# Bucketed quads of a graph network's scatter-add: 16 groups of 392 nodes in place of 8 of 784, four row bands of the matrix array at once, parts by truncation

## The chip, the cores and the metric

One core of a Trainium2 chip runs the whole program. The metric is the time of one execution on the device, in microseconds, as the median of several runs. The core has five engines with queues of their own: TensorE (PE in the profile; its weight loads are PEld), VectorE (DVE), ScalarE (ACT), GpSimd (POOL) and the queue that issues most DMAs, SyncE (SP). TensorE writes into PSUM, which is held here as eight banks of 128 x 512 float32: four under the tag A and four under the tag B.

## The reference, cut to what matters

6250 nodes with 128 features, 200000 edges sorted by `dst`. A layer norm and a relu, a matrix, then for each edge a filter from its 20 attributes, the product of that filter and the row of node `dst`, summed at node `src`; then two more matrices, and the input is added.

```python
h = jnp.maximum(_layernorm(x, axis=-1), 0.0)
x_in = h @ W_in
W_ij = shifted_softplus(f_ij @ W_f1 + b_f1) @ W_f2 + b_f2
W_ij = W_ij * f_ij_cutoff
x_ij = x_in[dst] * W_ij
out = jax.ops.segment_sum(x_ij, src, num_segments=N_ATOMS)
return x + shifted_softplus(out @ W_o1 + b_o1) @ W_o2 + b_o2
```

`src` is random over all nodes, so the sum over edges is the hard part: every edge adds a row of 128 float32 numbers at a random node.

## The kernel before

The edges are taken in quads: four chunks of 128 edges, 512 in all. There are 391 quads. One loop (from `s1_pe(0)` on, near line 903) runs over iterations i and issues, in an order written out by hand, one stage of each of several quads: the filter's first layer of quad i + 1, its softplus of quad i, the gather of node rows and the second layer of quad i - 1 (`xg`, `W`), the product `m` of i - 1, and the sum within each chunk of i - 2. Everything else is hung into that loop by `at(i, point, function)`; the points of an iteration are, in this order: L (loads), A0 (ScalarE), D0 (VectorE), D1 (VectorE), A1, then after the main products PE2 (TensorE), A2, D2 (VectorE) and S (scatters). Each engine works its own queue strictly in the order in which instructions were issued.

A quad's 512 rows of `m` reach their nodes in one of two ways.

A direct quad compares the edges of each chunk with each other (`s1_eq`, line 308), sums the rows of equal nodes by a float32 matmul (`s3_pe`, `pp`, line 356), copies the result (`s3_copy`, line 364), computes where to write (`s3_idx`), and scatters four times 128 rows into one of four accumulators in HBM by an indirect DMA that adds (`scatter`, line 399, issued by GpSimd).

A bucketed quad (`mpq`, every third quad from quad 5 on, 128 of them) is summed on TensorE without HBM. The nodes are cut into 8 groups of 784 (`GRP`, `GN`). `rank_group` to `rank_slot` give each edge of eight quads at a time a slot: its group's 64 slots (`CAP`) in order of rank, or one of 64 overflow slots (`OVC`). Then, for each quad:

- `m` is cut into three bfloat16 parts whose sum is `m`: `part_cast` (ScalarE, line 493) rounds `m`, `part_rem` (VectorE, line 499) takes the remainder, `part_cast` rounds that, `part_rem` (line 504) takes the rest. The parts and three columns for the node's place (`ext`) stand side by side in `pt`, 387 columns.
- `perm_oh` (line 485) makes the 0/1 matrix `pm` from edge to slot, `permute` (line 510) multiplies, in four blocks of 128 slots, and `perm_out` (ScalarE, line 517) copies each block from PSUM to `ms`.
- `over_pe` (lines 531 to 533) sums the parts of the edges in overflow slots, and for each two quads `over_idx` to `over_scatter` write these by one scatter.
- Four quads share an accumulation (`RND`). `unit_oh` (line 586) makes, for one block of slots, the 0/1 matrix from slot to place in the group (784 columns); `unit_pe` (line 601) multiplies each part of `ms` with it, for the block's two groups in two 64-row bands of the array, into two PSUM banks, in two halves h of 392 columns; `unit_evac` (lines 611 and 613, VectorE) adds each bank to `accT`, the sum over all bucketed quads in SBUF.

A half unit is 4 quads x 3 parts x 2 bands = 24 matmuls. The halves run at PE2 of iterations q + 5 and q + 6 of the next round's quads, and are added to `accT` at D0 of the iteration after. Permutes run at PE2 of q + 4 and q + 5, two blocks each.

Around the loop: the node table is built in small groups during the first 60% (`prep_*`), the attributes are split and written back to HBM (`fb_*`), and near the end the first accumulator is loaded, transposed and added to `accT` (`r0_load`, line 832, through tiles of the tag `pm`; `r0_tp`, line 839). After the loop the other three accumulators are loaded, summed and added, and the last two matrices follow (lines 1020 on).

A loop behind line 957 would redo edges that found no slot; its count of trips is computed on the chip, and it is 0 when every overflow fits.

Of the kernel before, what the change touches and what calls it, by code (L numbers as in the profile page):

```python
# [20 lines left out]
P = 128  # L21
SC = 1024
SEG = 512
GRP = 8
CAP = 64
# [3 lines left out]
MPGAPS = (3,)  # L29
MPEND = 4  # L30
RND = 4
RKQ = 8
PW = 388
# [9 lines left out]
def tile_gnn(ctx: ExitStack, tc: tile.TileContext, x, fB, cT, srcT, srcr, dstr, win_, wf1, wf2, bias, bo1c, wo1,  # L43
# [25 lines left out]
    HN = GN // 2  # L69
    mpq = sorted_quads(NQ)  # L70
    mpi = {q: n for n, q in enumerate(mpq)}
    scat = [0] * (NQ + 12)
# [45 lines left out]
    iot = cp.tile([P, GN], F16, name="iot")  # L118
# [171 lines left out]
    def s1_ln(q):  # L290
        l = wk.tile([P, 512], F32, tag="l", name="l")
        nc.scalar.activation(l, st[q]["e"], AF.Ln, bias=half, scale=0.5)  # L292
        st[q]["l"] = l
# [34 lines left out]
    def s2_pe_w(q):  # L328
        W = ps.tile([P, 4, P], F32, tag="A", name="W", bufs=4)
        nc.tensor.matmul(W.rearrange("p c f -> p (c f)"), ones3[:, :P], b2rep.rearrange("k c f -> k (c f)"),  # L330
                         start=True, stop=False)
        for c in range(4):
            nc.tensor.matmul(W[:, c, :], st[q]["a"][:, c * P:(c + 1) * P], w2, start=False, stop=(c == 3))  # L333
        st[q]["W"] = W
# [7 lines left out]
    def s2_m(q):  # L342
        m = ms[q % 3]
        nc.vector.tensor_tensor(m[:, :, :P], st[q]["W"], st[q]["xc"], op=ALU.mult)  # L344
        st[q]["m"] = m
# [63 lines left out]
    def rank_group(r):  # L409
# [16 lines left out]
        ext = wk.tile([P, 4 * RKQ, 3], BF16, tag="ext", name="ext")  # L426
        nc.vector.tensor_copy(ext[:, :nc4, 0], loc[:, :nc4])
        nc.vector.tensor_tensor(ext[:, :nc4, 1], loc[:, :nc4], ext[:, :nc4, 0], op=ALU.subtract)
        nc.vector.tensor_copy(ext[:, :nc4, 2], cnt[:, :nc4])
# [59 lines left out]
    def part_cast(q, k):  # L489
        if k == 0:  # L490
            mp.setdefault(q, {})["pt"] = wk.tile([P, 4, PW], BF16, tag="pt", name="pt")
        src_ = st[q]["m"][:, :, :P] if k == 0 else mp[q]["rem"]
        nc.scalar.copy(mp[q]["pt"][:, :, k * P:(k + 1) * P], src_)  # L493

    def part_rem(q, k):
        pt = mp[q]["pt"]
        if k == 1:
            rem = wk.tile([P, 4, P], F32, tag="rem", name="rem", bufs=1)
            nc.vector.tensor_tensor(rem, st[q]["m"][:, :, :P], pt[:, :, :P], op=ALU.subtract)
            mp[q]["rem"] = rem  # L500
            r, j = divmod(mpi[q], RKQ)
            nc.vector.tensor_copy(pt[:, :, 3 * P:3 * P + 3], rk[r]["ext"][:, 4 * j:4 * j + 4])
        else:
            nc.vector.tensor_tensor(pt[:, :, 2 * P:3 * P], mp[q]["rem"], pt[:, :, P:2 * P], op=ALU.subtract)
            del st[q]

    def permute(q, s):
        t = ps.tile([P, 512], F32, tag="B", name="pq", bufs=4)
        for c in range(4):
            nc.tensor.matmul(t[:, :3 * P + 3], mp[q]["pm"][:, c, s * P:(s + 1) * P], mp[q]["pt"][:, c, :3 * P + 3],  # L510
                             start=(c == 0), stop=(c == 3))
        mp[q]["q", s] = t

    def perm_out(q, s):
        if s == 0:
            mp[q]["ms"] = wk.tile([P, 4, PW], BF16, tag="ms", name="mst", bufs=2 * RND)
        nc.scalar.copy(mp[q]["ms"][:, s, :3 * P + 3], mp[q].pop(("q", s))[:, :3 * P + 3])  # L517

    def perm_loc(q):
        lo = wk.tile([P, 4], F32, tag="lo", name="lo", bufs=2 * RND)  # L520
        nc.vector.tensor_tensor(lo, mp[q]["ms"][:, :, 3 * P], mp[q]["ms"][:, :, 3 * P + 1], op=ALU.add)
        mp[q]["lo"] = lo

    def over_pe(q):
# [3 lines left out]
        for c in range(4):  # L528
            w = mp[q]["pm"][:, c, GRP * CAP:]
            pt = mp[q]["pt"][:, c]  # L530
            nc.tensor.matmul(o[:, :P + 3], w, pt[:, 2 * P:3 * P + 3], start=(c == 0), stop=False)  # L531
# [4 lines left out]
    def over_out(q):  # L536
        h = mpi[q] % 2 * OVC
        mo = mos[mpi[q] // 2 % 2]
        nc.scalar.copy(mo[h:h + OVC, :P + 3], mp[q].pop("po")[h:h + OVC, :P + 3])

    def over_idx(q):
        mo = mos[mpi[q] // 2 % 2]
        so = sp_.tile([P, 2], F32, tag="ovs", name="ovs", bufs=2)
        nc.vector.scalar_tensor_tensor(so[:, 0:1], mo[:, P + 2:P + 3], float(GN), mo[:, P:P + 1], op0=ALU.mult,
                                       op1=ALU.add)
        nc.vector.tensor_tensor(so[:, 1:2], so[:, 0:1], mo[:, P + 1:P + 2], op=ALU.add)
        dg = wk.tile([P, P], F32, tag="dg", name="dg", bufs=1)
        nc.vector.tensor_scalar(dg, idt, so[:, 1:2], None, op0=ALU.mult)
# [7 lines left out]
    def over_eq(q):  # L556
        eq = wk.tile([P, P], F32, tag="oeq", name="oeq", bufs=1)
        nc.vector.tensor_scalar(eq, mp[q].pop("row")[:, :P], mp[q]["so"][:, 1:2], None, op0=ALU.is_equal)  # L558
        mp[q]["eq"] = eq

    def over_sum(q):
        t = ps.tile([P, 512], F32, tag="B", name="osum", bufs=4)
        nc.tensor.matmul(t[:, :132], mp[q]["eq"], mos[mpi[q] // 2 % 2][:, :132], start=True, stop=True)
        mp[q]["sum"] = t

    def over_copy(q):
        s = sp_.tile([P, 132], F32, tag="os", name="os", bufs=2)
        nc.scalar.copy(s, mp[q].pop("sum")[:, :132])  # L568
        mp[q]["os"] = s

    def over_ji(q):
        s, so = mp[q]["os"], mp[q]["so"]
        jd = sp_.tile([P, 2], F32, tag="ojd", name="ojd", bufs=2)
        nc.vector.tensor_scalar(jd[:, 0:1], so[:, 1:2], trash, None, op0=ALU.subtract)
        nc.vector.scalar_tensor_tensor(jd[:, 1:2], s[:, 131:132], wgt2, jd[:, 0:1], op0=ALU.is_lt, op1=ALU.mult)
# [7 lines left out]
    def unit_oh(r, s):  # L583
        for q in mpq[r * RND:(r + 1) * RND]:
            so = wk.tile([P, GN], BF16, tag="so", name="so", bufs=RND + 1)
            nc.vector.tensor_scalar(so, iot, mp[q]["lo"][:, s:s + 1], None, op0=ALU.is_equal)  # L586
# [4 lines left out]
    def unit_pe(r, s, h):  # L591
        ts = []
        for g in range(2):
# [3 lines left out]
        for q in qs:  # L597
            for k in range(3):
                for g in range(2):
                    v = slice(g * CAP, (g + 1) * CAP)  # L600
                    nc.tensor.matmul(ts[g][:, :HN], mp[q]["ms"][v, s, k * P:(k + 1) * P],  # L601
                                     mp[q]["oh"][v, h * HN:(h + 1) * HN], start=(q == qs[0] and k == 0),
                                     stop=(q == qs[-1] and k == 2))
        un[r, s, h] = ts

    def unit_evac(r, s, h):
        for g, t in enumerate(un.pop((r, s, h))):
            o = (2 * s + g) * GN + h * HN
            v = accT[:, o:o + HN]
            if r == 0:  # L610
                nc.vector.tensor_copy(v, t[:, :HN])
            else:
                nc.vector.tensor_tensor(v, t[:, :HN], v, op=ALU.add)  # L613
# [19 lines left out]
    def src_cols(a, b):  # L633
        t_ = wk.tile([P, b - a], I32, tag="pt", name="srci")
        nc.sync.dma_start(t_, srcT[:, a:b])
        nc.gpsimd.tensor_copy(srcT_sb[:, a:b], t_)
# [6 lines left out]
    with tc.manual_schedule():  # L643
# [9 lines left out]
        nc.gpsimd.iota(iot, pattern=[[1, GN]], base=0, channel_multiplier=0, allow_small_or_imprecise_dtypes=True)  # L653
# [7 lines left out]
        src_cols(0, CE)  # L661
        nc.sync.dma_start(w2, wf2)
# [5 lines left out]
        ones3 = cp.tile([3, 512], BF16, name="ones3")  # L668
# [9 lines left out]
        def split3(dst, src, rows, c0, tag):  # L678
            p = wk.tile([rows, 3, P], BF16, tag="e", name=f"{tag}_parts")
            r = wk.tile([rows, P], F32, tag="l", name=f"{tag}_rem")  # L680
# [54 lines left out]
        for i in range(3):  # L735
# [3 lines left out]
        for mo_ in mos:  # L739
            nc.vector.tensor_copy(mo_[:, 131:132], wgt)  # L740
# [16 lines left out]
        def late_cols():  # L757
            w = -(-(EP // P - CE) // 2)
            src_cols(CE, CE + w)
            src_cols(CE + w, EP // P)  # L760
            nc.sync.dma_start(cT_sb[:, CE:], cT[:, CE:])

        at(3 if spread else 0, "D2", rel_ext, 0, rel0)
        if CE < EP // P:
            at(7, "L", late_cols)

        def half_piece(k, tag, **kw):
            lo, hi = k * SEG, (k + 1) * SEG
            r = rel(1, lo, hi, tag, **kw)
            src_cast(1, lo, hi, nc.vector, tag, **kw)  # L770
            rel_ext(1 + k, r)

        kw = {"bufs": 2 * RND}
        for k in range(2):
            i = 2 + 2 * k if spread else 0
            at(i, "L", lambda k=k: load_idx(1, k * SEG, (k + 1) * SEG, "ms", **kw))
            at(i + 2 if spread else i, "D2", lambda k=k: half_piece(k, "ms", **kw))
# [4 lines left out]
        for g in range(1, NG):  # L782
# [15 lines left out]
            at(t0 + 3, "D1", prep_rm, g)  # L798
# [57 lines left out]
        at(mid + 7 if spread else 0, "D1", late_add)  # L856
# [3 lines left out]
        for g in range(len(tgroups)):  # L860
# [3 lines left out]
            at(min(i + 3, NQ + 4), "D1", r0_add, g)  # L864
        for r in range(-(-len(mpq) // RKQ)):
            i = mpq[RKQ * r]
            at(i - 4, "D2", rank_group, r)
            at(i - 2, "PE2", rank_count, r)
            at(i - 1, "D1", rank_own, r)
            at(i, "PE2", rank_over, r)  # L870
            at(i + 1, "D1", rank_slot, r)
        for q in mpq:
            at(q + 2, "A2", part_cast, q, 0)
            at(q + 2, "D2", part_rem, q, 1)
            at(q + 2, "D2", perm_oh, q)
            at(q + 3, "A1", part_cast, q, 1)
            at(q + 3, "D2", part_rem, q, 2)
            for s in range(4):
                at(q + 4 + s // 2, "PE2", permute, q, s)
                at(q + 5 + s // 2, "A0", perm_out, q, s)  # L880
            at(q + 4, "PE2", over_pe, q)
            at(q + 5, "A0", over_out, q)
            at(q + 6, "D1", perm_loc, q)
            if mpi[q] % 2:
                at(q + 5, "D2", over_idx, q)
                at(q + 6, "PE2", over_row, q)
                at(q + 7, "D1", over_eq, q)
# [5 lines left out]
        for r in range(len(mpq) // RND):  # L893
            for u in range(8):
                s, h = divmod(u, 2)
                n = RND * (r + 1) + s
                k = (mpq[n] + 5 if n < len(mpq) else last + 7 + 2 * s) + h
                if h == 0:
                    at(k - 1, "D2", unit_oh, r, s)
                at(k, "PE2", unit_pe, r, s, h)  # L900
                at(k + 1, "D0", unit_evac, r, s, h)

        s1_pe(0)
        for i in range(max(NQ + 6, last + 16)):
# [54 lines left out]
    with tc.For_i(0, trips, 1) as ci:  # L959
# [10 lines left out]
        sb = wk.tile([P, P], I32, bufs=1, tag="rem", name="fsb")  # L970
# [27 lines left out]
        nc.tensor.matmul(W, ones3[:, :P], b2rep[:, 0, :], start=True, stop=False)  # L998
# [8 lines left out]
        s = wk.tile([P, P], F32, tag="l", name="fs")  # L1007
# [230 lines left out]
```

## Time and profile before

| | |
|---|---|
| median of 3 runs | 2316.84 us (2315.01 to 2321.35) |
| the profiled execution: time, span | 2317.84 us, 2315.7 us |
| mean granted TensorE clock | 0.974 |
| iterations of the loop | 391 and 11 that finish |
| scatters (line 399) | 1051 of direct quads, 64 of overflow |
| unit matmuls (line 601) | 6144 |
| permute matmuls (line 510) | 2048 |
| adds and copies to accT (lines 613, 611) | 496 and 16 |

A busy time is the union of an engine's instructions; the gap between two start times tells what an instruction costs its engine when the next one follows at once. [...]

### The profile page before, as it was taken

The numbers are of one execution on the slowest core, as the hardware profiler recorded it, in microseconds if no ns is written. First come the engines' busy times: TensorE is split into PE (matmuls) and PEld (weight loads), VectorE is DVE, ScalarE is ACT, GpSimd is POOL, SyncE is SP. The second block draws the span as 40 slices with busy tenths as digits, with TensorE's granted clock in tenths as the row PEclk, the third lists the DMA queues.
The fourth block names the chain that finished last, engine by engine and source line by source line (L and its number), as shares of the span: only waits on it lengthen the run. The fifth ranks groups of instructions, "written<-read, shape, count | busy, mean of one in ns | idle before, by whom it ended". The sixth has DMA issues, their size and how long they took to land.

```text
span 2315.7 us, 53016 instructions
## 1 busy us (share of the span) xinstructions
PE 2142.7 (93%) x18065; PEld 1492.7 (64%) x18065; DVE 1976.5 (85%) x5339; ACT 1843.1 (80%) x4486; POOL 1844.8 (80%) x1159
## 2 busy tenths in 40 slices
PE   4589999999999999999999999999999999999886
PEld 3466666666666666666666666666666666666554
DVE  6589888999989999998989889888888888898574
ACT  4498888888888888888888888878888888887534
POOL 3677788888888888888888888888888888887564
PEclk8699999999999999999999999999999999999997
DMA  8887777777777777777777777777777677776537
GB/s 302 210 185 140 143 145 149 145 143 152 151 142 137 160 146 140 151 146 150 138 155 142 135 141 145 148 133 141 134 145 141 140 147 140 140 147 136 117 41 222
DMA packets 399056, 345.26 MB, mean 149 GB/s; under 512 B 87656, under 2 KB 313806, under 8 KB 398784
## 3 DMA queue, kind: packets, MB, share of 16 engines
q1 hardware_dynamic: 237136, 265.37, 38.2%
q0 software_dynamic: 161360, 76.42, 33.8%
q8 instruction: 142, 2.33, 0.4%
q14 instruction: 130, 1.06, 0.2%
q10 hardware_dynamic: 288, 0.07, 0.0%
HBM read 198.15 MB, written 143.57 MB: 148 GB/s over the span
## 4 chain that ended last, share of the span: by engine, by line
PE 63%; ACT 20%; DVE 7%; DMA 4%; issue 3%; SPq 1%; POOL 1%; ACTq 0%; DVEq 0%; POOLq 0%
PE un L601 20%; PE W L333 11%; PE pp L356 9%; PE pq L510 8%; ACT xc L339 5%; PE xg L325 3%; PE W L330 3%; ACT e L287 3%; ACT e L286 3%; PE z L281 2%; ACT pt L493 2%; DMA acc<-s,ji 2%; PE po L531 2%; ACT l L292 2%; PE po L533 1%
## 5 line engine op out<-in xcount | busy, mean ns | idle before, releaser
L399 POOL DMA_INDIRECT acc<-s,ji x1051 | 1703.5, 1621 | 396.2 <-issue 177.3
L601 PE MATMUL un<-so,mst 64*128 64x392 bf16 x6144 | 597.1, 332 | 47.2 <-ACT os L568 17.7
L601 PEld LDWEIGHTS <-mst 64*128 64x128 bf16 x6144 | 321.3, 95 | 278.0 <-issue 95.3
L339 ACT ACTIVATE xc<-xg,cT_sb 128x128 f32<-128x128 f32 x1564 | 443.1, 363 | 52.1 <-PE xg L325 48.7
L333 PE MATMUL W<-w,a 128*128 128x128 f32 x3128 | 461.1, 291 | 0.0
L333 PEld LDWEIGHTS W<-w,a 128*128 128x128 f32 x3128 | 385.7, 194 | 93.4 <-issue 92.7
L510 PE MATMUL pq<-pt,pm 128*128 128x387 bf16 x2048 | 380.4, 327 | 1.0 <-DVE oeq L558 0.9
L314 DVE SCALAR_TENSOR_TENSOR a<-z,l 128x512 f32<-128x512 f32 x391 | 267.3, 684 | 80.3 <-ACT l L292 80.3
L344 DVE TENSOR_TENSOR m<-W,xc 128x512 f32<-128x512 f32 x391 | 267.1, 683 | 58.9 <-ACT xc L339 56.8
L364 ACT COPY s<-pp 128x258 f32<-128x258 f32 x526 | 192.4, 382 | 156.0 <-PE pp L356 142.8
L613 DVE TENSOR_TENSOR accT<-un,accT 128x392 f32<-128x392 f32 x496 | 256.2, 557 | 62.7 <-PE un L601 60.0
L356 PEld LDWEIGHTS pp<-m,eq 128*128 128x128 f32 x2104 | 283.7, 196 | 13.5 <-ACT s L364 2.0
L292 ACT ACTIVATE l<-e,con 128x512 f32<-128x512 f32 x391 | 282.2, 722 | 12.7
L356 PE MATMUL pp<-m,eq 128*128 128x129 f32 x2104 | 284.6, 279 | 1.4 <-ACT s L364 1.4
L517 ACT CAST mst<-pq 128x387 bf16<-128x387 f32 x512 | 238.7, 502 | 59.3 <-PE pq L510 59.2
L510 PEld LDWEIGHTS <-pm 128*128 128x128 bf16 x2048 | 198.4, 97 | 115.6 <-issue 1.7
L287 ACT ACTIVATE e<-e 128x512 f32<-128x512 f32 x391 | 246.5, 630 | 12.5
L286 ACT ACTIVATE e<-z 128x512 f32<-128x512 f32 x391 | 241.7, 618 | 9.4 <-PE z L281 7.9
L586 DVE TENSOR_SCALAR so<-iot,lo 128x784 bf16<-128x784 f16 x512 | 192.4, 437 | 0.1
L485 DVE TENSOR_SCALAR pm<-iot,pos 128x576 bf16<-128x576 f16 x512 | 165.7, 385 | 22.5 <-PE rtp L839 22.5
L308 DVE TENSOR_TENSOR eq<-sb,srcT_sb 128x512 f32<-128x512 int16 x263 | 179.1, 681 | 0.0
L325 PE MATMUL xg<-wn,oh 126*128 126x128 bf16 x1564 | 157.5, 224 | 16.1 <-DVE a L314 10.4
(157 smaller groups left out, 2567.4 us busy)
## 6 DMA issues: line engine op xcount, KB each, us to landing
sb<-src SPq DMA_DIRECT2D x195, 256.0 KB
rb<-reld SPq DMA_DIRECT2D x195, 252.0 KB
ft<-fsd SPq DMA_DIRECT2D x195, 240.0 KB
fsd<-f SPq DMA_DIRECT2D x49, 480.0 KB
acc<-s,ji POOLq DMA_INDIRECT x1051
fb<-in_fB_dram SPq DMA_DIRECT2D x49, 320.0 KB
fsd<-f SPq DMA_DIRECT2D x49, 320.0 KB
wn<-tab SPq DMA_DIRECT2D x391, 31.5 KB
```

Of the source, the lines that this page charges most:

```text
L286: nc.scalar.activation(e, st[q]["z"], AF.Abs)
L287: nc.scalar.activation(e, e, AF.Exp, scale=-1.0)
L292: nc.scalar.activation(l, st[q]["e"], AF.Ln, bias=half, scale=0.5)
L314: nc.vector.scalar_tensor_tensor(a, st[q]["z"], 0.0, st[q]["l"], op0=ALU.max, op1=ALU.add)
L333: nc.tensor.matmul(W[:, c, :], st[q]["a"][:, c * P:(c + 1) * P], w2, start=False, stop=(c == 3))
L339: nc.scalar.mul(xc[:, c, :], st[q]["xg"][:, c, :], cT_sb[:, 4 * q + c:4 * q + c + 1])
L344: nc.vector.tensor_tensor(m[:, :, :P], st[q]["W"], st[q]["xc"], op=ALU.mult)
L356: nc.tensor.matmul(pp[:, c, :129], st[q]["eq"][:, k, :], m[:, k, :129], start=True, stop=True)
L399: nc.gpsimd.indirect_dma_start(out=accs[k][:, :], out_offset=bass.IndirectOffsetOnAxis(ap=ji, axis=0), in_=s, in_offset=None, compute_op=A ...
L510: nc.tensor.matmul(t[:, :3 * P + 3], mp[q]["pm"][:, c, s * P:(s + 1) * P], mp[q]["pt"][:, c, :3 * P + 3], start=(c == 0), stop=(c == 3))
L601: nc.tensor.matmul(ts[g][:, :HN], mp[q]["ms"][v, s, k * P:(k + 1) * P], mp[q]["oh"][v, h * HN:(h + 1) * HN], start=(q == qs[0] and k == 0) ...
L613: nc.vector.tensor_tensor(v, t[:, :HN], v, op=ALU.add)
```

## The change

It touches the bucketed quads, how many there are, and the buffers around them.

- 16 groups of 392 nodes with 32 slots each (`GRP`, `CAP`); a block of 128 slots holds four groups, so a unit multiplies four bands of 32 rows into four PSUM banks at once, all four under the tag B. There are no halves.
- Three quads of eight are bucketed (gaps 3, 2, 3): 144. Six quads share an accumulation, so there are 24 rounds of four units, each 6 x 3 x 4 = 72 matmuls of 392 columns.
- Parts by truncation: `m` of a bucketed quad is written straight into a float32 `pt`; the upper 16 bits of a float32 are its truncated bfloat16, so a part is a view of every second bfloat16 of the float32 tile (`high`). ScalarE's two casts are gone; the two remainders stay on VectorE and write float32. The moving operand of `permute` and `over_pe` has a step of two elements.
- A node's place in its group needs one column in place of two (it is stored less 196, and 196 is added back in `perm_loc` and `over_ji`), so `ext` has two columns and `pt` 386.
- `perm_oh` runs at q + 1 (before q + 2), both remainders at q + 2, permutes at q + 3 and q + 4 (before q + 4 and q + 5), `perm_loc` in two halves; units run at q + 2 of those quads of the next round that follow at a gap of three, an iteration in which the direct product `pp` is missing because quad q is bucketed.
- Rank steps run one iteration apart and some of them move from D1 to D0, as do `over_eq`, `prep_rm`, `late_add` and `r0_add`.
- `l` is written over `e`; two `m` buffers instead of three; the late halves of the indices are loaded through the tag `pm` at iterations 1 and 2 (before 2 and 4) and cast at 3 and 5 (before 4 and 6); two late blocks of `srcT` are loaded at iterations 11 and 13 (before both at 7) and narrowed by VectorE (before GpSimd).

```diff
-GRP = 8
-CAP = 64
+GRP = 16
+CAP = 32
-MPGAPS = (3,)
+MPGAPS = (3, 2, 3)
-RND = 4
+RND = 6
-PW = 388
+PW = 386
...
     def s2_m(q):
-        m = ms[q % 3]
+        m = part_new(q) if q in mpi else ms[plain[q] % 2]
...
-    def part_cast(q, k):
-        if k == 0:
-            mp.setdefault(q, {})["pt"] = wk.tile([P, 4, PW], BF16, tag="pt", name="pt")
-        src_ = st[q]["m"][:, :, :P] if k == 0 else mp[q]["rem"]
-        nc.scalar.copy(mp[q]["pt"][:, :, k * P:(k + 1) * P], src_)
+    def high(t):
+        return t.bitcast(BF16)[:, :, 1::2]
+
+    def part_new(q):
+        mp.setdefault(q, {})["pt"] = wk.tile([P, 4, PW], F32, tag="pt", name="pt")
+        return mp[q]["pt"]
 
     def part_rem(q, k):
         pt = mp[q]["pt"]
+        a = pt[:, :, (k - 1) * P:k * P]
+        nc.vector.tensor_tensor(pt[:, :, k * P:(k + 1) * P], a, high(a), op=ALU.subtract)
...
-            nc.tensor.matmul(t[:, :3 * P + 3], mp[q]["pm"][:, c, s * P:(s + 1) * P], mp[q]["pt"][:, c, :3 * P + 3],
+            nc.tensor.matmul(t[:, :PW], mp[q]["pm"][:, c, s * P:(s + 1) * P], high(mp[q]["pt"][:, c:c + 1, :PW])[:, 0],
                              start=(c == 0), stop=(c == 3))
...
-    def unit_pe(r, s, h):
+    def unit_pe(r, s):
         ts = []
-        for g in range(2):
+        for g in range(4):
             t = ps.tile([P, 512], F32, tag="B", name="un", bufs=4)
             ts.append(t)
         qs = mpq[r * RND:(r + 1) * RND]
         for q in qs:
             for k in range(3):
-                for g in range(2):
+                for g in range(4):
                     v = slice(g * CAP, (g + 1) * CAP)
-                    nc.tensor.matmul(ts[g][:, :HN], mp[q]["ms"][v, s, k * P:(k + 1) * P],
-                                     mp[q]["oh"][v, h * HN:(h + 1) * HN], start=(q == qs[0] and k == 0),
-                                     stop=(q == qs[-1] and k == 2))
+                    nc.tensor.matmul(ts[g][:, :GN], mp[q]["ms", s // 2][v, s % 2, k * P:(k + 1) * P], mp[q]["oh"][v],
+                                     start=(q == qs[0] and k == 0), stop=(q == qs[-1] and k == 2))
...
         for r in range(len(mpq) // RND):
-            for u in range(8):
-                s, h = divmod(u, 2)
-                n = RND * (r + 1) + s
-                k = (mpq[n] + 5 if n < len(mpq) else last + 7 + 2 * s) + h
-                if h == 0:
-                    at(k - 1, "D2", unit_oh, r, s)
-                at(k, "PE2", unit_pe, r, s, h)
-                at(k + 1, "D0", unit_evac, r, s, h)
+            nxt = [mpq[n] + 2 for n in range(RND * (r + 1), min(RND * (r + 2), len(mpq))) if mpq[n] - mpq[n - 1] == 3]
+            for s in range(4):
+                k = nxt[s] if nxt else last + 6 + 2 * s
+                at(k - 1, "D2", unit_oh, r, s)
+                at(k, "PE2", unit_pe, r, s)
+                at(k + 1, "D0", unit_evac, r, s)
```

## The prediction

> **What bounds the kernel now.** I read the page first, then the busy time by stage, then TensorE's and VectorE's timelines. All sums below stand against the profiled execution: span 2315.7 us, 2317.84 us as a time, 1.0 us above the median 2316.84.
>
> ```profile
> span 2315.7 us, 53016 instructions
> PE 2142.7 (93%) x18065; PEld 1492.7 (64%) x18065; DVE 1976.5 (85%) x5339; ACT 1843.1 (80%) x4486; POOL 1844.8 (80%) x1159
> PE 63%; ACT 20%; DVE 7%; DMA 4%; issue 3%; SPq 1%; POOL 1%; ACTq 0%; DVEq 0%; POOLq 0%
> ```
>
> ```profile
> 0.00:150.00 150.00, 87.21 (x531) 66.36 (x532) 92.38 (x257) 88.27 (x218) 84.32 (x69) 0.83 0.85 241
> 150.00:2100.00 1950.00, 1882.78 (x16220) 1309.23 (x16218) 1746.66 (x4763) 1644.15 (x4022) 1629.19 (x1004) 0.99 0.73 145
> 2100.00:2316.00 216.00, 172.73 (x1319) 117.07 (x1318) 137.40 (x323) 110.64 (x248) 131.27 (x88) 0.90 0.59 125
> ```
>
> The columns are length, then busy time of PE, PEld, DVE, ACT, POOL. From 150 to 2100 us PE is busy 1882.78/1950 = 96.6%, DVE 89.6%, ACT 84%, POOL 84%: TensorE sets the pace, VectorE is 136 us behind it, and the granted clock is 0.99. Busy overcounts streaming, but start times agree:
>
> ```profile
> 1002.00 2.17 PE L601 MATMUL un<-so,mst 64*128 64x392 bf16 x24
> 1004.10 0.40 PE L325 MATMUL xg<-wn,oh 126*128 126x128 bf16 x4
> ...
> 1005.96 1.05 PE L356 MATMUL pp<-m,eq 128*128 128x129 f32 x8
> 1006.85 1.48 PE L510 MATMUL pq<-pt,pm 128*128 128x387 bf16 x8
> 1008.27 0.24 PE L531 MATMUL po<-pt,pm 128*64 128x131 bf16 x1
> ...
> 1009.06 0.40 PE L325 MATMUL xg<-wn,oh 126*128 126x128 bf16 x4
> ```
>
> From start to next start: half a unit (24 matmuls) takes 2.10 us, the product pp 0.89, two permuted slot blocks 1.42, the overflow block 0.79. In the first, two 64-row bands take 12 x 175 ns for 392 columns; a full-height permute of 387 columns takes 1.42/8 = 177 ns. So the second band costs nothing beside the first.
>
> **TensorE, part by part.**
> - Accumulation: 256 half units x 2.10 = 537.6 us go. 96 units of 72 matmuls come, in 18 groups of four row bands. Two bands already stream at the price of one, so I give four the same 175 ns: 3.15 us a unit, 302.4 in all, **-235**. Ends: no dearer than that, or two bands at a time, 36 x 175 = 6.30 us, 604.8 in all (+67). I take the first, the nearer row being two bands that overlap wholly.
> - 16 more bucketed quads x (2 x 1.42 + 0.79) = **+58**; 16 fewer direct products x 0.89 = **-14**.
> - Ranks 16 to 18 groups at twice the width, and 8 more overflow pairs: at most **+12** (orow and osum are busy 26.8 + 25.0 us for 64 now, so 0.8 us a pair).
> - The permutes now read every second bf16 of a float32 tile. No row has a strided moving operand. Ends: nothing, or half the stream rate, 144 x (16 x 177 ns + 12 x 66 ns) = +522. The nearest row is pp, whose float32 operand has a 4-byte step too and takes 0.89/8 = 111 ns a row of 129 columns against 66 ns for bf16 po; but it does other arithmetic and comes as two instructions a product, so it decides little. I take nothing.
>
> Sum **-179**, to 1964 us.
>
> [...]
>
> **VectorE.**
>
> ```profile
> 1008.33 1.41 DVE L586 TENSOR_SCALAR so<-iot,lo 128x784 bf16<-128x784 f16 x4
> 1009.66 0.21 DVE L379 SCALAR_TENSOR_TENSOR jf<-s,con,jd 128x4 f32<-128x4 f32 x1
> ...
> 1013.73 0.68 DVE L499 TENSOR_TENSOR rem<-m,pt 128x512 f32<-128x512 f32 x1
> 1014.33 0.17 DVE L502 COPY pt<-ext 128x12 bf16<-128x12 bf16 x1
> 1014.40 1.20 DVE L485 TENSOR_SCALAR pm<-iot,pos 128x576 bf16<-128x576 f16 x4
> 1015.52 1.03 DVE L613 TENSOR_TENSOR accT<-un,accT 128x392 f32<-128x392 f32 x2
> 1016.47 0.34 DVE L299 TENSOR_SCALAR oh<-rb,con 126x512 bf16<-126x512 bf16 x1
> ```
>
> By starts: so 1.33/4 = 0.333 us at 784 columns, pm 1.12/4 = 0.28 at 576, so 392 columns cost 0.28 - 184 x 0.000255 = 0.233; an accT add 0.475; a remainder 0.60.
> - accT 512 to 384: **-61**. so 512 x 0.333 to 576 x 0.233: **-36**.
> - Remainders 256 to 288: **+19**; pm +64 x 0.28 = **+18**; lo 128 to 288 at 0.16: **+25**; eq and index work of 16 quads at 0.60 + 0.38: **-16**.
> - Ranks: five operations widen by 256 elements, 0.27 us each (0.60 against 0.475 for 120 columns); 18 x 1.33 and two groups of 5 us more: **+34**. Overflow and narrowing srcT on DVE instead of POOL: **+4**.
>
> Sum **-13**: VectorE is not relieved.
>
> **ScalarE and GpSimd.**
>
> ```profile
> L493 ACT CAST pt<-m 128x512 bf16<-128x512 f32 x128 | 80.6, 630 | 23.8 <-POOL srcT_sb L636 23.8
> L493 ACT CAST pt<-rem 128x512 bf16<-128x512 f32 x128 | 77.6, 607 | 24.1 <-DVE rem L499 24.1
> ```
>
> Both casts go (-158), 64 more mst copies come (238.7/512 each, +30), s loses 32 of 0.37 (-12), others +5: ACT **-135**. Scatters fall from 1115 to 987 + 72 = 1059: at 1.62 us **-91** on POOL. Both lie beside TensorE and are worth nothing alone; without that cover each ACT microsecond would be paid.
>
> **What is late next.** In the middle stage PE loses its share of 179, some 172, to 1711 us; DVE stays near 1735. So VectorE ends last, by a hair. At the 96.6% that PE reaches now, DVE would need 1796 us for the 1950 (-154). But two engines 1.4% apart wait on each other in turn, and the order adds a coupling: a unit takes all four B banks of PSUM. It is queued where no pp is due (two iterations after a quad), so its banks wait only for ACT's last copies of pq and po (2 x 0.47 + 0.26 = 1.2 us), under xg, W, z (1.86 us, from 1004.10 to 1005.96). Behind the unit on PE stand the next xg, W, z, again 1.86 us, then pp, which waits for the first of four accT adds (1.9 us in all), first in DVE's next iteration. Cover and need are about equal, so a late DVE now stops PE. I take 95%: 1735 / 0.95 = 1826, **-124**.
>
> Moved steps: half_load's four DMAs on SP go one and three iterations earlier and late_cols' two source columns four to six later, their copy passing from POOL's queue to DVE's; SP spends 0.35 to 0.5 us on an issue (sb, rb, ft in its timeline), under zeroing transfers and table loads that fill those iterations; I price this at nothing, 2 us without that cover. At the end accs[0] comes back through tiles that share tag pm, and pm now lives from q+1 to q+4 instead of q+2 to q+4; its issue already blocks SP:
>
> ```profile
> 2119.35 15.85 SPq L832 DMA_DIRECT2D r0t<-acc  x2
> ```
>
> 0 to +20 for that; I take **+5**, as only some of the 13 loads meet a pm. Span 2315.7 - 124 + 5 = 2197, as a time 2199, against the median **2198**. Own range: DVE at 98% (-180) gives 2135, DVE at 92% (-64) with +20 gives 2271.
>
> **Rivals.**
> - D, TensorE stays the bound with its whole gain: 2316 - 179 + 5, **2142**. For it: PE reaches 96.6% today with DVE at 90%. Against: DVE's unchanged sum.
> - C, the four-bank unit turns into a wait. If DVE comes 0.8 us late at each of 96 units, PE stands 77 us: 2198 + 77 = **2275**. For it: PE un already ends 60.0 us of DVE idle time at L613, so they run in step. Against: all hooks sit where a pp is missing.
> - A, on the other side: the stride slows the permutes. At half rate 2316 - 179 + 522 = **2659**; it decides from a permute of 177 + 179/2304 us, 255 ns. For it: no row shows such a read. [...]
> - B, bands run two at a time: 604.8 - 302.4 more, **2440**; decides from 279 ns a group. Against: the wholly hidden second band.
> - The drop path (an edge over a full bucket starts the repair loop) doesn't start: counted over the inputs, a bucketed quad has at most 57 edges over 32 in its group, and 64 places for them.
>
> **How the numbers follow.** Main 0.68, D 0.08, C 0.13, A 0.07, B 0.04. Predicted 2198. The range 2130 to 2285 takes in the main case's ends, D and most of C, some 0.82. A measurement tells 0.3% (7 us) from no change. Faster 0.87 (main, D, nearly all of C), same 0.02, slower 0.11 (A, B).
>
> **What would show it.** Starts of un four at a time, some 175 ns apart, a unit of 3.1 to 3.3 us (B: 6.3); pq still 177 ns (A: over 255); DVE busy 1950 to 1980 us at 93% or more in the middle stage, ACT near 1710; PE's idle time ended by DVE (accT, a) where it hardly is today. I am wrong in the step "late next" if PE stays over 96% busy there, or DVE falls below 90% with the time above 2250.

## The result and the profile after

The changed kernel takes 2335.43 us (median of 5 runs, 2332.85 to 2342.51) against 2318.31 us for the kernel before (5 runs as well): ratio 1.008, 95% interval 1.0061 to 1.01. It is slower by 17 us, where 120 us less were forecast. The profiled execution has a span of 2331.0 us. The head of its profile and the busy time by stage of the changed kernel (columns as before: PE, PEld, DVE, ACT, POOL, then the granted clock):

```profile
span 2331.0 us, 55463 instructions
PE 2009.1 (86%) x19201; PEld 1405.5 (60%) x19201; DVE 1946.9 (84%) x5586; ACT 1706.7 (73%) x4286; POOL 1728.0 (74%) x1101
PE 45%; DVE 30%; ACT 11%; DMA 6%; issue 5%; SPq 1%; POOL 1%; DVEq 0%; ACTq 0%; POOLq 0%
```

```profile
150.00:2100.00 1950.00, 1744.72 (x17145) 1220.53 (x17143) 1703.54 (x4940) 1501.27 (x3795) 1518.94 (x951) 0.96 0.71 141
2100.00:2331.00 231.00, 163.76 (x1436) 111.18 (x1433) 135.97 (x344) 109.30 (x252) 129.53 (x87) 0.86 0.59 122
```

Every engine is busy for less time than before, and none fills the middle stage: TensorE is busy 89% of it (it was 96.6%), VectorE 87%. VectorE's share of the chain of work that ended last rose from 7% to 30%, TensorE's fell from 63% to 45%. That fits two engines that take turns, and the timelines below show them do it.

The costs of the pieces came out close to the forecast. TensorE's timeline, first a unit that starts undisturbed, then two permutes of two blocks each:

```profile
1119.42 3.16 PE L598 MATMUL un<-so,mst 32*128 32x392 bf16 x72
1122.52 0.40 PE L325 MATMUL xg<-wn,oh 126*128 126x128 bf16 x4
```

```profile
1010.81 1.54 PE L508 MATMUL pq<-pt,pm 128*128 128x386 bf16 x8
1012.19 0.39 PE L325 MATMUL xg<-wn,oh 126*128 126x128 bf16 x4
...
1014.04 1.54 PE L508 MATMUL pq<-pt,pm 128*128 128x386 bf16 x8
1015.51 0.24 PE L530 MATMUL po<-pt,pm 128*64 128x130 bf16 x1
```

From start to next start a unit takes 3.10 us (predicted 3.15), 3.10/18 = 172 ns a group of four: four bands run at the price of one. The permute with its step of two takes 1.38/8 = 172 ns a matmul where `xg` follows. The 177 ns of the kernel before were read where `po` follows, 1.42 us for eight, and there the new permute takes 1.47. From start to start inside such a run of eight the median is 164 ns before and 173 ns now: the step of two is cheap, but not free. Of the 96 units 43 have no small product just ahead of them in the queue, and 38 of these start undisturbed. Most of the others do not:

```profile
1029.51 0.34 PE L598 MATMUL un<-so,mst 32*128 32x392 bf16 x3
1034.40 5.22 PE L598 MATMUL un<-so,mst 32*128 32x392 bf16 x69 [4.55 <-DVE rt L472]
1039.55 0.40 PE L325 MATMUL xg<-wn,oh 126*128 126x128 bf16 x4
```

Three of the four bands start, the fourth stands 4.55 us, and then the unit streams for 5.2 us instead of 2.84 (the time from its first to its last start where nothing stands). Just ahead of it, in the same PE2, stands a product of the rank steps, `rko`. Tag B is a ring of four banks: a unit's four tiles take the banks of the last four tiles issued, whatever these were, and `rko` is the last. Its reader is VectorE, at D0 of the next iteration. VectorE's timeline shows how far it was from there:

```profile
1031.26 0.68 DVE L344 TENSOR_TENSOR m<-W,xc 128x512 f32<-128x512 f32 x1
1031.86 0.68 DVE L498 TENSOR_TENSOR pt<-pt 128x512 f32<-128x512 f32 x1
1032.46 0.26 DVE L501 CAST pt<-ext 128x8 f32<-128x8 bf16 x1
1032.58 0.69 DVE L498 TENSOR_TENSOR pt<-pt 128x512 f32<-128x512 f32 x1
...
1034.15 0.19 DVE L472 SCALAR_TENSOR_TENSOR rt<-rko,ov 128x32 f32<-128x32 f32 x1
...
1039.95 1.98 DVE L609 TENSOR_TENSOR accT<-un,accT 128x392 f32<-128x392 f32 x4 [5.08 <-PE xg L325]
```

VectorE first works off the iteration, reads `rko` for the last time at 1034.15, and after 0.5 us of small work has nothing to do until the unit is through (5.08 us; `xg`, which is named there, follows the unit at once). Busy time by stretch of the same place, with the granted clock in the column after POOL:

```profile
1024.00:1029.50 5.50, 5.38 (x48) 3.84 (x46) 5.43 (x20) 4.81 (x13) 3.24 (x3) 1.00 0.65 146
1029.50:1034.40 4.90, 0.35 (x7) 0.10 (x4) 4.62 (x16) 3.72 (x9) 4.29 (x3) 0.73 0.45 40
1034.40:1039.60 5.20, 5.20 (x70) 2.49 (x71) 0.47 (x5) 0.00 (x0) 4.29 (x4) 0.59 0.43 39
1039.60:1044.00 4.40, 4.40 (x35) 3.41 (x35) 4.05 (x9) 2.54 (x8) 0.63 (x1) 1.00 0.22 20
```

First TensorE stands while VectorE works, then VectorE stands while TensorE works, at a granted clock of 0.59. The waits of the whole run (total, times, longest):

```profile
ACT xc L339 <- PE xg L325: 258.7, 53, 11.4
...
DVE accT L609 <- PE un L598: 113.1, 26, 5.8
...
PE un L598 <- DVE pr L448: 56.6, 10, 6.9
...
PE un L598 <- DVE so L583: 32.4, 23, 3.2
...
PE un L598 <- DVE rt L472: 31.4, 10, 4.8
...
PE un L598 <- DVE rm L211: 23.3, 7, 5.4
PE un L598 <- DVE accT L852: 22.7, 7, 6.0
```

The readers are those of the small products: pr and rt of the ranks, rm of the node table, accT L852 of the first accumulator's return. (The last releaser is named; so L583 stands for a wait that ended near it.) From the start times of all unit matmuls, the 96 units stand some 200 us together (170.9 us in gaps of over 0.6 us inside them, some 30 us ahead of their first matmuls), and stream 331.8 us where 96 x 2.84 would be 272.6: some 260 us on TensorE's own queue.

### The profile page after: what moved, and what is told of

The parts are those of the page before. It is cut to its first block, busy times and chain, and to the rows that moved or that the text cites. A ratio compares the mean times of both kernels' runs of the same rounds, so it can differ in the third digit from the quotient of the medians.

```text
span 2331.0 us, 55463 instructions
## 1 busy us (share of the span) xinstructions
PE 2009.1 (86%) x19201; PEld 1405.5 (60%) x19201; DVE 1946.9 (84%) x5586; ACT 1706.7 (73%) x4286; POOL 1728.0 (74%) x1101
## 4 chain that ended last, share of the span: by engine, by line
PE 45%; DVE 30%; ACT 11%; DMA 6%; issue 5%; SPq 1%; POOL 1%; DVEq 0%; ACTq 0%; POOLq 0%
PE pq L508 10%; PE un L598 10%; PE W L333 8%; PE pp L356 6%; DMA acc<-s,ji 4%; DVE so L583 4%; DVE pm L484 4%; ACT xc L339 3%; DVE pt L498 3%; DVE a L314 3%; PE W L330 2%; PE xg L325 2%; DVE eq L308 2%; DVE m L344 2%; ACT e L287 2%
## 5 line engine op out<-in xcount | busy, mean ns | idle before, releaser
L399 POOL DMA_INDIRECT acc<-s,ji x987 | 1573.9, 1595 | 526.4 <-issue 170.5
L598 PE MATMUL un<-so,mst 32*128 32x392 bf16 x6912 | 381.1, 365 | 186.2 <-DVE pr L448 56.6
L508 PE MATMUL pq<-pt,pm 128*128 128x386 bf16 x2304 | 452.5, 335 | 27.7 <-ACT s L364 15.2
L598 PEld LDWEIGHTS <-mst 32*128 32x128 bf16 x6912 | 206.8, 103 | 344.4 <-issue 159.4
L516 ACT CAST mst<-pq 128x386 bf16<-128x386 f32 x576 | 271.8, 500 | 95.9 <-PE pq L508 79.5
L314 DVE SCALAR_TENSOR_TENSOR a<-z,e 128x512 f32<-128x512 f32 x391 | 267.4, 684 | 70.4 <-ACT e L292 43.4
L292 ACT ACTIVATE e<-e,con 128x512 f32<-128x512 f32 x391 | 282.2, 722 | 12.7
L609 DVE TENSOR_TENSOR accT<-un,accT 128x392 f32<-128x392 f32 x368 | 182.2, 557 | 125.8 <-PE un L598 113.1
L498 DVE TENSOR_TENSOR pt<-pt 128x512 f32<-128x512 f32 x288 | 198.6, 689 | 0.0
L344 DVE TENSOR_TENSOR m<-W,xc 128x512 f32<-128x512 f32 x247 | 168.3, 681 | 13.1 <-ACT xc L339 6.2
```

The source lines that it names most:

```text
L292: nc.scalar.activation(e, e, AF.Ln, bias=half, scale=0.5)
L314: nc.vector.scalar_tensor_tensor(a, st[q]["z"], 0.0, st[q]["l"], op0=ALU.max, op1=ALU.add)
L399: nc.gpsimd.indirect_dma_start(out=accs[k][:, :], out_offset=bass.IndirectOffsetOnAxis(ap=ji, axis=0), in_=s, in_offset=None, compute_op=A ...
L498: nc.vector.tensor_tensor(pt[:, :, k * P:(k + 1) * P], a, high(a), op=ALU.subtract)
L508: nc.tensor.matmul(t[:, :PW], mp[q]["pm"][:, c, s * P:(s + 1) * P], high(mp[q]["pt"][:, c:c + 1, :PW])[:, 0], start=(c == 0), stop=(c == 3))
L516: nc.scalar.copy(mp[q]["ms", a][:, b], mp[q].pop(("q", s))[:, :PW])
```

## The experiments

**The rank steps moved.** Units stand at iterations `uit`; a rank product that falls on one goes an iteration earlier.

```diff
-            at(i - 4, "D2", rank_group, r)
-            at(i - 3, "PE2", rank_count, r)
-            at(i - 2, "D0", rank_own, r)
-            at(i - 1, "PE2", rank_over, r)
-            at(i, "D0", rank_slot, r)
+            a, b = i - 3, i - 1
+            a -= a in uit
+            b -= b in uit
+            at(a - 1, "D2", rank_group, r)
+            at(a, "PE2", rank_count, r)
+            at(a + 1, "D0", rank_own, r)
+            at(b, "PE2", rank_over, r)
+            at(b + 1, "D0", rank_slot, r)
```

> The changed kernel with one thing moved: the rank steps' two TensorE products (and their VectorE readers) go one iteration earlier wherever they stood in an iteration with a unit. Theory T (a unit's four tiles take the whole ring of four B banks, so its last tile waits for the VectorE reader of the small product issued just ahead of it, which stands at the head of VectorE's next iteration): in the profile of the changed kernel the 17 units behind a rank product lose 108 us in standing and, at some 4.9 us of streaming instead of 2.84, another 35 us. T expects these waits gone and 2190 to 2230 us. Rival V (VectorE is simply late through its own load, and the wait only shows at the unit): the waits move to other lines and the time stays at 2320 to 2340 us.

Measured: 2247.98 us, ratio to the kernel before 0.9699 (0.9668 to 0.973). The units stand some 120 us in place of 200 and stream 303.4 in place of 331.8, some 110 us less, of which the time shows 87. T's direction is right, its amount too large by 20 to 60 us: the units with no product just ahead, 58 of them now, stand 22 us together, where the 43 of before stood 2. That fits the moved products' readers, which now head VectorE's queue in the unit's own iteration. V expected 2320 or more and falls.

**All small products moved.** Besides that, the overflow sum of the quads whose `q + 8` is in `uit` goes one iteration later, the node table's groups start where neither their transposes nor their products meet a unit, and the first accumulator's return uses iterations without a unit.

```diff
+                k = q + late1[q]
-                at(q + 8, "PE2", over_sum, q)
+                at(k + 8, "PE2", over_sum, q)
...
+    while g > 1 and t % 8 in (0, 1, 5, 6):
+        t += 1
...
-            i = ret_at + 3 + g
+            i = [k for k in range(ret_at + 5, NQ + 12) if k not in uit][g] - 2
```

> As the run before, and every other small product of tag B (overflow sum, node table's transposes and products, the transposes of the first accumulator at the end) is kept out of the iterations with a unit too. T: all units start their four tiles together and stream in 2.84 us from first to last start; 200 us of standing and 59 us of slow streaming are at stake, VectorE's 1947 us then set the end: 2110 to 2170 us, granted clock back at 0.97 or more. V: above 2290 us.

Measured: 2208.08 us, ratio 0.952 (0.9487 to 0.9553); 127 us under the changed kernel. Nothing is computed otherwise; only the order differs. The profile's granted clock is 0.973 (0.948 in the changed kernel). T's range ended at 2170, so it is missed by 38 us: the standing was the main loss, but VectorE's busy time alone does not set what is left. Its middle stage, and the waits that remain:

```profile
150.00:2050.00 1900.00, 1774.12 (x17578) 1237.46 (x17576) 1749.53 (x5042) 1542.38 (x3890) 1553.88 (x970) 0.99 0.75 149
```

```profile
PE pp L358 <- DVE accT L611: 43.0, 42, 2.4
...
PE un L600 <- DVE so L585: 13.9, 15, 3.0
PE un L600 <- DVE pr L450: 12.7, 10, 1.5
```

TensorE is at 93.4%, VectorE at 92.1%: level, as foreseen, at less than the 95% that was assumed.

**The rank products in a bank of tag A**, the order untouched: a second way to free the unit from them.

```diff
-        t = ps.tile([P, 512], F32, tag="B", name="rkp", bufs=4)
+        t = ps.tile([P, 512], F32, tag="A", name="rkp", bufs=4)
...
-        t = ps.tile([P, 512], F32, tag="B", name="rko", bufs=4)
+        t = ps.tile([P, 512], F32, tag="A", name="rko", bufs=4)
```

> The changed kernel in its own order, with the rank products in a bank of tag A instead of tag B. T: the units behind a rank product no longer stand, though nothing was moved, and the time falls nearly as far as with the rank steps moved, 2190 to 2250 us (tag A's ring shifts by one tile, worth 20 us at most). V, or an explanation by where the rank steps' VectorE work lies: 2320 to 2340 us.

Measured: 2279.74 us, ratio 0.9829 (0.9794 to 0.9863). The 15 units with only a rank product ahead now stand less than 1 us together (some 95 in the changed kernel), with everything in its old place. So it is the bank and not where the work lies. The time falls by 56 us, less than T's 85 to 145: the ring of tag A pays for the tile. Its trace shows waits that the changed kernel's has not, of the rank products themselves and of `z`, which shares tag A, for the rank's reader:

```profile
PE rkp L433 <- ACT xc L339: 15.2, 13, 1.8
...
PE rko L433 <- ACT xc L339: 9.1, 7, 1.3
PE rko L433 <- DVE a L314: 8.8, 9, 2.8
PE z L281 <- DVE pr L448: 8.8, 9, 2.2
```

These four make 42 us, where T allowed tag A 20.

**Truncation alone**, in the kernel before: float32 `pt`, operands by `high`, no `part_cast`; 8 groups of 64 slots, 128 quads, two bands and halves as they were. To make room, `l` is written over `e` here too, and a few temporary tiles share other buffers.

```diff
-        m = ms[q % 3]
+        m = part_new(q) if q in mpi else ms[q % 3]
...
-            at(q + 2, "A2", part_cast, q, 0)
-            at(q + 3, "A1", part_cast, q, 1)
```

> The kernel before with the parts by truncation alone: float32 parts, operands read with a step of two, no casts on ScalarE; groups, slots, bands, quads as before. T and the prediction: the permutes keep 177 ns, ScalarE loses some 158 us of busy time off the path, the time stays within 15 us of the kernel before (2300 to 2325 us). If the truncated parts were part of what the change lost: 2330 us or more.

Measured: 2303.04 us, ratio 0.9927 (0.9899 to 0.9954): a gain of 17 us. ScalarE's busy time falls from 1843.1 to 1710.9 us. A permute's median step rises from 164 to 171 ns, at the same 387 columns: the step of two costs TensorE some 13 us here (256 runs of eight, 1.42 to 1.47 us each), and the gain holds all the same. The parts by truncation alone are no part of the loss.

**VectorE relieved**, on top of all small products moved: `lo` and the copy of `ext` on ScalarE.

```diff
-        nc.vector.tensor_scalar(lo, mp[q]["ms", a][:, :, 3 * P], float(GN // 2), None, op0=ALU.add)
+        nc.scalar.activation(lo, mp[q]["ms", a][:, :, 3 * P], AF.Identity, bias=con[:, 14:15])
...
-            nc.vector.tensor_copy(pt[:, :, 3 * P:PW], rk[r]["ext"][:, 4 * j:4 * j + 4])
+            nc.scalar.copy(pt[:, :, 3 * P:PW], rk[r]["ext"][:, 4 * j:4 * j + 4])
```

> The kernel with all small products moved, and two small VectorE jobs given to ScalarE: the 288 place columns (lo, 0.195 us each in the listing) and the 144 copies of ext. The question is the prediction's step 'what is late next': with the bank waits gone, does VectorE end last? If it does (theory V2), some 65 us off VectorE's path move the time from 2208 to 2145 to 2180 us, while ScalarE, at 78%, takes 80 us more. If TensorE or the order between engines sets the end (theory P2), the time stays within 15 us of 2208.

Measured: 2239.74 us, ratio 0.9658 (0.9642 to 0.9674): 32 us slower than without it. VectorE's busy time falls from 1953.7 to 1922.2 us and ScalarE's rises from 1711.2 to 1802.2. V2 falls for this move, and P2's 15 us is missed on the other side. The waits that grew, from 24.2, 7.8 and nothing in the kernel with all moved to, here:

```profile
PE pq L510 <- ACT s L366: 40.5, 50, 2.4
...
PE po L532 <- ACT s L366: 15.4, 26, 0.6
...
PE pq L510 <- ACT xc L341: 8.9, 9, 1.2
```

Together they rose by 33 us, as much as the time. ScalarE frees the banks of tag B too, and the two jobs were put ahead of some of that work. What VectorE's relief alone would bring, without ScalarE's load, this run does not show.

**One quad in three** (126) instead of three in eight, all else as with all moved.

```diff
-MPGAPS = (3, 2, 3)
+MPGAPS = (3,)
...
-    while g > 1 and t % 8 in (0, 1, 5, 6):
+    while g > 1 and t % 3 != 1:
```

> The kernel with all small products moved, and bucketed quads one in three (126) instead of three in eight (144); 21 rounds of four units. By the rows of the changed kernel 18 quads less take from TensorE 18 x 3.63 + 12 units x 3.0 - 18 x 0.89 = 85 us and from VectorE some 80 us, and bring 63 more scatters on GpSimd, 100 us, to 1835 us. If the larger share of bucketed quads is a cost now (T2): 2130 to 2180 us. If GpSimd's scatters or the transfers behind them take the place (rival G): 2200 us or more.

Measured: 2276.61 us, ratio 0.9808 (0.9787 to 0.9829). T2 falls: in this order the larger share of bucketed quads is worth having. G's number fits, and a wait for scattered rows is there that was 3.2 us with all moved,

```profile
ACT s L366 <- DMA acc<-s,ji: 41.9, 19, 5.8
```

but pp's wait for accT rose as well, from 43.0 to 75.2 us, and the granted clock fell to 0.929. How the 68 us divide between these stays open.

**Stricter order.** A small product that VectorE reads also stays out of the iteration before a unit's.

```diff
-            a -= a in uit
-            b -= b in uit
+            while b + 1 in uit or b in uit:
+                b -= 1
+            a = min(a, b - 1)
+            while a + 1 in uit or a in uit:
+                a -= 1
```

> As the kernel with all small products moved, and stricter: a small product whose reader is VectorE also stays out of the iteration before a unit's, so that no such reader is queued at the head of the unit's own iteration. In the profile of that kernel units still wait 13 us for pr, 8 for rt, 4 for oeq, 14 for so, with slow streaming behind some. If these small waits are what is left of theory T's cause (S): 2175 to 2195 us. If VectorE's own lateness at the unit's adds (pp waits 43 us for accT there) rules (L): 2200 to 2215 us.

Measured: 2207.99 us, ratio 0.9537 (0.952 to 0.9554), the same as with all moved. The units' standing falls from some 53 to 25 us, pp's wait for accT rises from 43.0 to 62.1. L's number holds, and its account fits: most of the wait moved to the next place where VectorE is due.

**The second remainder later.**

```diff
-            at(q + 2, "D2", part_rem, q, 2)
+            at(q + 3, "D1", part_rem, q, 2)
```

> As the run before, and the second remainder (0.6 us on VectorE) goes behind the unit's four adds, from the end of iteration q + 2 to iteration q + 3. L: the adds start 0.6 us earlier at most units, pp waits less for accT, and the time falls by 15 to 45 us against the run before. Rival: the permutes, which need that part in the same iteration, wait in pp's place (pq waiting for pt), and the time stays within 10 us of the run before or rises.

Measured: 2235.4 us, ratio 0.9653 (0.9636 to 0.967), 27 us slower than the run before. The rival is right; the waits of this kernel:

```profile
PE pq L511 <- DVE pt L501: 66.6, 80, 2.3
...
PE pp L359 <- DVE accT L612: 28.4, 31, 1.8
```

pp waits 34 us less for accT than in the run before (62.1), and pq waits 67 us for the part (2.0 there), 0.8 us in the mean at 80 places.

## Why the prediction was wrong

The step that failed is in "what is late next", as the prediction put it: a unit "is queued where no pp is due (two iterations after a quad), so its banks wait only for ACT's last copies of pq and po". pp, pq and po were counted as users of tag B, and the small ones were not: rank counts, overflow sum, node table, first accumulator. One of them stands just ahead of 51 of the 96 units. Where VectorE is the reader, the unit can wait for most of an iteration of VectorE's (4.55 us in the stretch shown), because such a reader stands at D0 of the next one. In the kernel before, a unit took two banks of the ring, so a product just ahead of it had two tiles of grace; there the waits of all half units make 47 us, and 7 us of them name VectorE. The prediction's own sign of this failure came: VectorE below 90% of the middle stage with the time above 2250.

Rival C had the mechanism and a wrong size and place: 0.8 us at each unit, 77 us. Measured were some 200 us of standing, unevenly (4 to 9 us behind a rank product, mostly 1.3 us behind an overflow sum, 2 us in all at the 43 units with no small product ahead), and 59 us of slow streaming, a term the prediction did not have at all. With the small products out of the way the time is 2208.08 us, 10 us from the 2198 forecast for an order without these waits. That this is so near is partly luck: the stretch of quads that fills the middle stage of the kernel before takes 1867 us there, where 1826 were forecast, and the start and the end together are some 32 us shorter than before, where 5 more were forecast.

Point by point:
- Four bands at the price of one: right, 3.10 us a unit against 3.15. A group of four follows every 166 ns (17 steps in an undisturbed unit), where one full-height permute of 386 columns takes 173 ns; rival B needed 279 ns.
- The strided operand is free: nearly right. The 177 ns to compare with was 1.42/8, which has the longer step to `po` in it. Like for like it is 164 ns before and 173 now, some 17 us over the 288 runs of eight. The sum put them at nothing, an estimate of the author's: no run had shown such a read. Rival A needed 255 ns.
- TensorE 1964 us: busy 2009.1 with the slow streaming, 1986.5 with all moved. VectorE unchanged at some 1964: 1946.9. ScalarE -135: -136.4. GpSimd -91: -116.8.
- VectorE ends last "by a hair" at 95%: half right. Both engines are at 92% to 93% with most of these waits gone. Relieving VectorE at ScalarE's cost lost 32 us. Whether VectorE alone sets what is left stays open.
- Rivals A and B: ruled out by the rows above. D was not reached.

## What to carry to other kernels

When a consumer takes more tiles of a rotating set of banks, list every tile that the same queue takes from the set just before it, the smallest too, and ask who frees each and how far from there that engine is. A wait of one engine for another's next iteration can cost twice: once on each side, as in the stretch shown (TensorE 4.55 us, then VectorE 5.08 us). Move such a product out of that iteration before anything else is tuned; here it was worth 127 us with no change to the work.

## What the runs showed of the hardware

Behind a long stand the clock was lower as well. In the changed kernel, units that stood 2.3 us or less in all streamed in 2.8 to 3.4 us (one, behind 1.57 us, took 4.5 us), those that stood 3.2 us or more in 4.1 to 5.8 us. In the stretch shown the granted clock was 0.73 while TensorE stood, 0.59 in the 5.2 us after, and 1.00 again from then on. What lowers the clock was not shown.

Four 32-row bands into four PSUM banks ran at the price of one: a group of four matmuls of 392 columns every 166 ns, as a pair of 64-row bands did in the kernel before. A bfloat16 moving operand read with a step of two from a float32 tile cost 171 to 173 ns a matmul of 386 or 387 columns, a packed one 164 ns.
